# A layer-0 and attention kernel on one core: TensorE's first, middle and last step from searched lists, group two's layer-0 products among the first norms, and one due time for the last chains

## The chip, the cores and the metric

One Trainium2 chip, of which the kernel uses one core. The metric is the device time of one execution in microseconds (us); less is better. All arithmetic is fp32. A core has TensorE (PE in the profile; PEld is its weight load), VectorE (DVE), ScalarE (ACT), GpSimd (POOL) and SyncE (SP, which issues the DMAs here). TensorE writes into PSUM, which has eight banks of 128 x 512 fp32 numbers; the other engines read and write them too.

## The reference

The input x holds 128 graphs of 128 nodes with 512 features. adj is one 128 x 128 matrix, the same for all graphs, with many zeros.

```python
# layer 0
A = einsum('od,bdn->bon', adj, x);  C = A + b[None, :, None]
x = layernorm(x + max(relu(A[:, :, None, :] + (C - A)[:, :, :, None]), axis=-1))
# layer 1: 8 heads of 64
q, k, v = split(x @ w_qkv)
p = softmax(where(adj == 0, -inf, q @ k.T / 8))
o = (p @ v) @ w_proj + b_proj
x = layernorm(x + o + layernorm(o) * ln_gamma + ln_beta)
```

In layer 0 the maximum over the last axis comes down to one number for each node: the largest entry of its row of adj @ x, plus its bias, and no less than 0. So layer 0 costs a product, a row maximum and a norm for each graph.

## The kernel before

**Tiling.** The 128 graphs make 32 groups (`NG`) of `G` = 4. A step p of the main loop (L1297) works on four groups at once (p-1 to p+2), in a software pipeline. Its parts, by the letters that the changed program's lists use too:

- A0 to A3 (`attend`, L1156): probabilities times V for the four graphs of group p-1; ScalarE copies each result out of its bank (L1177).
- S0 to S3 (`scores`, L1034, and `softmax`, L1053): scores of the four graphs of group p, two banks for each graph. VectorE adds the mask and takes the maximum, ScalarE makes eight exponentials (L1087, one for each head, with the row sums) and eight scalings by 1/sum (L1116). Where `on_vector` is true, VectorE scales instead. VectorE transposes in 32 x 32 pieces (L1128), and a DMA out to a DRAM tile (`hop`) and one DMA in for each of four quarters finish the transposition.
- V1 to V7 and O1 to O7 (`Unit`, L880): the V projection of group p and the output projection of group p-1, as Strassen-like schemes of seven products of half size. GpSimd makes four sums of the left operand first. Products add up in four banks; between them ScalarE takes snapshots of a bank (`u`, L919), and VectorE combines bank and snapshot into the result. O's banks 0 and 2 start from a copy of the bias by ScalarE (`seed`).
- L0 to L3 (`l0_mm`, L444): layer-0 products adj @ x of group p+2, each with a row maximum on VectorE; after them come the group's statistics (`bn`, L464), roots and shifts (`finish`, L469, GpSimd), the norm on ScalarE (`norm`, L531), the transposition of x through VectorE and DRAM (`xhop`), and the spill of x with beta added.
- Q0 to Q25 (`qk_unit`, L772): q and k of group p+1, by a bilinear scheme of 26 products (`NODES`). GpSimd makes sums of x (`token_sums`) for it. Between products ScalarE copies a bank into another that goes on from there (a seed, L806) or into a snapshot (L810), and VectorE and GpSimd combine at the end.
- `tails` (L1200): for group p-1, both layer norms, the residual and the store, with x reloaded from the spill.

**The first step** (L1248 to L1295) is written out: layer 0 of group 0, here called I0 to I3, with a norm for each graph; TensorE transposes of its x (X0 to X3, `l0_transpose_pe`, L603), each copied out by ScalarE or VectorE; its q and k by plain products (D0 to D7, `qk_plain`, L719, 16 matmuls each); the layer-0 products of group 1, here J0 to J3; and fillers (`keep_warm`, L365: matmuls on zeros whose result nobody reads). **The last step** (L1351 to L1461) is written out as well: there is no next group, so the attentions of the last group (here B0 to B3), the plain output projection of its graphs (`project`, L1419, here R0 to R3, four 128 x 512 matmuls each on a bank that `seed_last` has filled with the bias) and the chains behind (`tail_before`, L1392, for graphs of the group before, here T0 to T3; `tail`, L1429; both end in `outer`, L1408: statistics, roots on GpSimd, norm on ScalarE, store) close the program.

**TensorE's order** is that of the calls. Before the change it is:

```
first:  K3 T K1 I0 K1 I1 K1 I2 K1 I3 K2 X0 X1 D0 D1 D2 D3 X2 X3 J0 J1 D4 D5 J2 J3 D6 D7 S0 S1 S2 S3
        V1 V2 L0 L1 V6 V5 V4 V7 L2 L3 V3 Q0 ... Q25
middle: A0-A3 S0-S3 V1 V2 L0 L1 V6 L2 L3 V5 V4 V7 O1 O2 V3 O6 O5 O7 O4 Q0 Q1 O3 Q2 ... Q25
last:   A0-A3 S0-S3 V1 V2 V6 V5 V4 V7 O1 O2 V3 O6 O5 O4 O7 B0 O3 B1 T0 R0 B2 T1 R1 B3 T2 R2 T3 R3
```

(K with a number: that many fillers; the first K3 and T, the transpose of adj, are the same in both programs. The Ts in the last row put no work on TensorE; they stand where their chains are added to the plan.)

**The other engines' order** comes from `Plan` (L160). Every operation is recorded with its engine, a cost and what it reads and writes. `schedule` (L221) goes backwards from TensorE and gives each operation a due time: the latest end that leaves its successors in time. An operation without a successor (a store, mostly) is due 9.0 (`BEHIND`) after the planned start of the TensorE operation that was added last before it. Then each engine takes, of what is ready, what is due first. SP's queue, the DMA issues, is ordered in the same way. The program is emitted in that order, and each engine runs its own instructions in it.

**Banks** are assigned by hand: lists X and Y of four banks change places through `FREED` (L131), `Unit` has a table `BANK`, and each row of `NODES` names its bank. A product into a bank waits until whoever reads the old content is done. Snapshots of the q/k scheme go to the buffers u0 to u5 by a table (`SNAP`, L133).

Of the kernel before, what the change touches and what calls it, by code (L numbers as in the profile page):

```python
# [2 lines left out]

# [78 lines left out]
    (((8, 0),), 0, 3, (2,), (), None),  # L82
    (((12, 1),), 2, 6, (), (19,), None),
    (((14, 2),), 1, 4, (8,), (), None),
    (((1, 3), (10, 4)), 0, 5, (), (7,), None),
    (((5, 5), (15, 6)), 1, 9, (7,), (), None),
    (((9, 7),), 0, 25, (10,), (), None),
    (((11, 8),), 2, 14, (12,), (), None),
    (((17, 9),), 4, 11, (20,), (), None),
    (((13, 10),), 3, 13, (), (16,), None),  # L90
    (((16, 11),), 1, 17, (), (12,), None),
    (((18, 12),), 5, 19, (), (11,), None),
    (((19, 13),), 4, 16, (), (15,), None),
    (((5, 14),), 6, None, (), (), 6),
    (((20, 15),), 3, 23, (18,), (), None),
    (((7, 16),), 2, 15, (), (19,), None),
    ((), 2, None, (), (), 7),
    (((6, 17),), 4, None, (), (), 4),
    (((21, 18),), 1, 21, (), (24,), None),
    (((22, 19),), 6, 22, (), (25,), None),  # L100
    (((23, 20),), 5, None, (), (), 3),
    (((24, 21),), 7, 24, (), (22,), None),
    (((0, 22),), 1, None, (), (23, 22), None),
    ((), 6, None, (), (), 1),
    (((25, 23),), 3, None, (), (), 5),
    (((1, 24),), 7, None, (), (), 2),
    (((2, 25),), 0, None, (), (), 0),
# [23 lines left out]
FREED = [2, 4, 5, 6, 1, 3, 7, 0]  # L131

SNAP = {1: 0, 3: 1, 8: 2, 9: 3, 10: 4, 11: 5, 14: 1, 17: 4, 18: 3, 20: 5, 21: 2}  # L133
# [26 lines left out]
class Plan:  # L160
# [32 lines left out]
    ROUNDS, KEPT, BEHIND = 6, 0.5, 9.0  # L193
# [27 lines left out]
    def schedule(self, ideal):  # L221
        ops = self.ops
        for op in reversed(ops):
            ahead = op.lag + (self.AHEAD_DMA + 1.5 * op.kb / self.KB_PER_US if op.kb else self.AHEAD)
            if op.succs:
                due = min(s.due - (0.0 if s.eng == op.eng == "PE" else ahead) for s in op.succs)
            else:
                due = ideal.get(op.after, 0.0) + self.BEHIND
            if op in ideal:
                due = min(due, ideal[op] + op.cost)  # L230
# [61 lines left out]
def kernel(  # L292
# [43 lines left out]

    def halves(b):
        return b.t.rearrange("p (k n) -> p k n", k=2)
# [24 lines left out]
    idle = bank(7)  # L363

    def keep_warm(n):  # L365
        def emit():
# [3 lines left out]
        plan.add("PE", 0.43 * n, emit, [zeros], [idle])  # L370

# [39 lines left out]
    load(2)  # L411
    load(3)
# [15 lines left out]
    pt0 = bank(6)  # L428
    plan.add("PE", 0.4, lambda: pin(PE.transpose(pt0.t[:, :P], adj_sb.t, ident.t)), [adj_sb, ident], [pt0])
    adj_done = plan.add("DVE", 0.25, lambda: pin(V.tensor_copy(adjT.t, pt0.t[:, :P])), [pt0], [adjT])  # L430
    mask = buf("mask", [P, P])
# [12 lines left out]
    def l0_mm(f, k):  # L444
        b = bank(k)
# [16 lines left out]
        )  # L462

# [139 lines left out]
    def l0_transpose_pe(f, k):  # L603
        g, c4 = divmod(f, G)
        h, j = divmod(c4, 2)
        b = bank(k)
# [8 lines left out]
        for half in range(2):  # L615
# [10 lines left out]
            else:  # L626
                plan.add("DVE", 0.4, lambda ops=operands: pin(V.tensor_copy(*ops())), [b], at)

# [18 lines left out]
    def block(i):  # L647
        k, n = divmod(i, 4)
        return raw[n], lambda: raw[n].t[:, k]

    def weight_forms():
        made = {}
        room = ("z", "xr0", "xr1")
        temp_bufs = [buf(s, [P, 4, HE]) for s in room]

        def operand(i):
            if i < 16:
                b, ap = block(i)
                return b, None, ap
# [33 lines left out]
        for w, terms in enumerate(FORMS):  # L693
# [3 lines left out]
            dst, at = (lambda w=w: wqk.t[:, w]), (wqk, w)  # L697
            if len(terms) == 1:
                (i, s), = terms
# [4 lines left out]
                    lambda ap=ap, dst=dst, s=s: pin(A.mul(dst(), ap(), float(s))),  # L704
# [6 lines left out]
            add(dst, at, operand(i), operand(j), si, sj)  # L711
            for i, s in terms[2:]:
                add(dst, at, (wqk, w, dst), operand(i), 1, s)

    def qk_bufs(g):
        for h in range(2):
            qk[g, h] = buf(f"qk{h}", [P, 4, 2, HT])

    def qk_plain(h, banks, eng, ns):  # L719
# [787 lines left out]
```

## Time and profile before

| | |
|---|---|
| device time, median of 3 runs | 1888.86 us (1888.54 to 1889.1) |
| profiled execution, device time | 1889.46 us |
| its span, first to last instruction | 1887.7 us |
| granted TensorE clock, mean | 0.997 |
| TensorE busy | 1865.2 us (99%), 11299 instructions |
| VectorE, ScalarE, GpSimd busy | 1328.0, 1484.1, 1543.4 us (70, 79, 82%) |
| moved by DMA | 341.89 MB, 181 GB/s |
| TensorE busy in 0 to 20 us | 17.52 of 20 (DMA share 0.95) |
| TensorE busy in 60 to 100 us | 36.82 of 40 |
| TensorE busy in 1700 to 1800 us | 100.00 of 100 |
| TensorE busy in 1860 to 1888 us | 12.99 of 28 (granted clock 0.82) |

Rows of the profile read like this. A group's row has the line of the code, the engine, the operation, `out<-in` by tile names (k is a bank, u a snapshot, hl and x1T operands of the projections, s probabilities), the shapes, and how many. In a timeline a row begins with its start and its length in us and gathers neighbours of one form (`x32`); brackets at its end hold the idle time before it and what ended that, as in `[1.39 <-ACT k L806]`: 1.39 us idle until ScalarE's copy of line 806 into k was there. The chain of waits is followed back from the last instruction, at each step to what released it. A table of windows has one row for each stretch: its length, then the busy time (and instructions) of PE, PEld, DVE, ACT and POOL, the granted clock, the DMA share and GB/s. L353 stands for every matmul, L347 and L350 for GpSimd's and VectorE's additions. A 128 x 256 fp32 matmul leaves two records on TensorE, 0.2155 us apart.

### The profile page before, as it was taken

To read this page: it belongs to the slowest core of one execution; us is meant where nothing else is said; L and a number is where in the kernel's file an instruction comes from. 1 tells how busy PE (TensorE), PEld (TensorE's weight loads), DVE (VectorE), ACT (ScalarE), POOL (GpSimd) and SP (SyncE) were. 2 spreads that over 40 slices of the span, in tenths; PEclk is the share of its full clock that TensorE was granted. 3 is DMA by queue.
4 is the path that set the end of the run, shared out by engine and by line. 5 is a ranking of instruction groups with operands and counts; after the bars stand their busy time and mean duration, and the time that the engine had idled before them with its cause. 6 is when DMAs were issued, how large, how long until landed. Compare 5 with 4: busy or idle time off the path is not lost.

```text
span 1887.7 us, 35406 instructions
## 1 busy us (share of the span) xinstructions
PE 1865.2 (99%) x11299; PEld 1592.8 (84%) x11299; DVE 1328.0 (70%) x2432; ACT 1484.1 (79%) x4377; POOL 1543.4 (82%) x1600
## 2 busy tenths in 40 slices
PE   9999999999999999999999999999999999999996
PEld 7788888888888888888888888888888888888884
DVE  6967766776766777667767667676676776776667
ACT  2677778987778877788878798787887878888875
POOL 5668988889888888888797888878888888888884
PEclk9999999999999999999999999999999999999998
DMA  6765677557675666766576756668575766757554
GB/s 210 181 179 130 180 212 201 153 166 192 183 219 165 171 172 180 211 191 155 172 184 192 208 146 190 172 190 213 159 184 160 201 190 190 174 155 198 173 185 156
DMA packets 444857, 341.89 MB, mean 181 GB/s; under 512 B 276736, under 2 KB 378240, under 8 KB 444672
## 3 DMA queue, kind: packets, MB, share of 16 engines
q1 hardware_dynamic: 444384, 339.11, 64.9%
q8 instruction: 91, 1.49, 0.3%
q14 instruction: 94, 0.77, 0.1%
q10 hardware_dynamic: 288, 0.52, 0.1%
HBM read 172.82 MB, written 166.72 MB: 180 GB/s over the span
## 4 chain that ended last, share of the span: by engine, by line
PE 96%; ACT 1%; POOL 1%; DVE 1%; issue 0%; DMA 0%; SPq 0%; POOLq 0%; ACTq 0%
PE k L353 96%; ACT s L1116 0%; ACT s L1087 0%; POOL rs L347 0%; DVE st L466 0%; ACT k L806 0%; DMA s<-hop 0%; SPq L357 0%; POOL x L347 0%; POOL hl L347 0%; ACT z L537 0%; POOL rs L478 0%; ACT u L810 0%; POOL sh L486 0%; DVE pu L1128 0%
## 5 line engine op out<-in xcount | busy, mean ns | idle before, releaser
L353 PE MATMUL k<-hl,wqk 128*128 128x256 f32 x2232 | 517.7, 379 | 1.4 <-ACT k L806 1.4
L353 PEld LDWEIGHTS k<-hl,wqk 128*128 128x128 f32 x2232 | 423.6, 190 | 60.4 <-issue 2.5
L1087 ACT ACTIVATE s<-s,nm 128x128 f32<-128x128 f32 x1024 | 397.1, 391 | 76.4 <-DVE nm L1078 72.9
L1116 ACT ACTIVATE s<-s,rec 128x128 f32<-128x128 f32 x992 | 312.5, 392 | 0.0
L347 POOL TENSOR_TENSOR hl<-x1T 128x512 f32<-128x512 f32 (+1 forms) x250 | 216.6, 874 | 81.4 <-PE k L353 73.1
L353 PE MATMUL k<-x1T,wqk 128*128 128x256 f32 x992 | 244.8, 379 | 3.0 <-ACT u L810 1.6
L350 DVE SCALAR_TENSOR_TENSOR qk<-k,u 128x512 f32<-128x512 f32 x248 | 169.9, 688 | 109.5 <-PE k L353 73.4
L810 ACT COPY u<-k 128x512 f32<-128x512 f32 x341 | 195.6, 584 | 58.9 <-PE k L353 33.9
L353 PE MATMUL k<-wv,hl 128*128 128x256 f32 x1024 | 241.4, 379 | 0.0
L353 PEld LDWEIGHTS k<-wv,hl 128*128 128x128 f32 x1024 | 194.5, 190 | 52.2 <-issue 16.7
L353 PE MATMUL k<-wp,so 128*128 128x256 f32 x992 | 224.5, 379 | 0.0
L353 PEld LDWEIGHTS k<-x1T,wqk 128*128 128x128 f32 x992 | 188.3, 190 | 29.3 <-ACT u L810 2.0
L350 DVE SCALAR_TENSOR_TENSOR s<-k,mask 128x512 f32<-128x512 f32 x256 | 158.3, 683 | 77.8 <-PE k L353 75.1
L353 PEld LDWEIGHTS k<-wp,so 128*128 128x128 f32 x992 | 188.4, 190 | 25.7 <-issue 0.2
L347 POOL TENSOR_TENSOR hl<-x1T,hl 128x512 f32<-128x512 f32 (+1 forms) x249 | 197.5, 807 | 0.2 <-DMA x1T<-xhop 0.2
L1087 ACT ACTIVATION_READ_ACCUMULATOR s<-s,nm 128x1 f32 x1024 | 194.3, 190 | 0.0
L919 ACT COPY u<-k 128x512 f32<-128x512 f32 x189 | 110.6, 586 | 101.7 <-PE k L353 96.1
L347 POOL TENSOR_TENSOR x<-x,be_bc 128x1024 f32<-128x1024 f32 x62 | 146.4, 2361 | 46.4 <-DVE xt L572 27.2
L353 PE MATMUL k<-wv,x1T 128*128 128x256 f32 x768 | 179.5, 383 | 0.0
L1128 DVE STREAM_TRANSPOSE pu<-s 128x1024 f32<-128x1024 f32 x128 | 158.2, 1236 | 27.1 <-ACT s L1116 27.0
L353 PE MATMUL k<-wp,oT 128*128 128x256 f32 x744 | 170.7, 379 | 0.0
L347 POOL TENSOR_TENSOR z<-z,ga_bc 128x1024 f32<-128x1024 f32 x60 | 142.0, 2366 | 29.1 <-ACT z L537 29.1
(138 smaller groups left out, 3366.6 us busy)
## 6 DMA issues: line engine op xcount, KB each, us to landing
hop<-pu SPq DMA_DIRECT2D x128, 512.0 KB, 2.7
s<-hop SPq DMA_DIRECT2D x512, 128.0 KB, 3.7
spill<-x SPq DMA_DIRECT2D x62, 512.0 KB, 4.8
xhop<-xt SPq DMA_DIRECT2D x248, 128.0 KB, 2.8
x1T<-xhop SPq DMA_DIRECT2D x248, 128.0 KB, 4.9
x<-in_x_dram SPq DMA_DIRECT2D x60, 512.0 KB, 5.1
xr<-spill SPq DMA_DIRECT2D x60, 512.0 KB, 5.3
out_dram<-xr SPq DMA_DIRECT2D x60, 512.0 KB, 5.1
```

Source lines behind the costliest of these rows:

```text
L347: pin(eng.tensor_tensor(dst, a, b, op))
L350: pin(V.scalar_tensor_tensor(dst, a, s, b, op0, op1))
L353: pin(PE.matmul(dst, lhsT=lhsT, rhs=rhs, start=start, stop=True, skip_group_check=True))
L810: plan.add("ACT", 0.5, lambda b=b, u=u: pin(A.copy(u.t, b.t)), [b], [u])
L919: plan.add("ACT", 0.5, lambda: pin(A.copy(u.t, b.t)), [b], [u])
L1087: A.activation(flat()[:, i], flat()[:, i], AF.Exp, bias=nm.t[:, i : i + 1], accum_out=sm.t[:, i : i + 1],)
L1116: A.activation(flat()[:, i], flat()[:, i], AF.Identity, scale=rec.t[:, i : i + 1])
L1128: V.transpose(u.t.rearrange("p q h b -> p h q b"), flat().rearrange("p h (q a) -> p h q a", q=Q),)
```

## The change

The three orders become lists that a search produced; one loop over all 32 steps reads them token by token. `FIRST` is step 0 (K, I, J, X, D, S, V, L, Q), `STEP` the middle steps (steps whose group p+2 doesn't exist drop their L), `LAST` step 31 (A, S, V, O, B, T, R). Each token is added to the plan where it stands, with all that hangs on it: S with its softmax, T and R with their chains, and `tails(p - 1)` right after O3. J0 to J3, layer 0 of the second group, now stand between the products, norms and transposes of the first (I, X, D0, D1). There are 6 fillers in place of 9, the three ahead of T included.

Banks are no longer named: `take` hands out the one that has been free longest, and `give` returns a bank as soon as the last reader is recorded. `NODES` loses its bank column, `SNAP` becomes a queue of the six buffers, `Unit` becomes `Strassen` (each product brings its snapshot and results, in any order), `qk_unit` becomes `Bilinear`. In the last step the bias copy into R's bank is added with each R, where before all four stood ahead of B0.

In `schedule` an operation without a successor that would be due within `EQUAL` = 12.0 of the end is due at the end (TensorE's planned end + 9.0), the same for all of these. The outer norm of the last graph goes to VectorE (`on_vector`: GpSimd makes only the root; one VectorE instruction subtracts the mean and multiplies), where the others have a shift on GpSimd and a norm on ScalarE. The loads of x for pairs 2 and 3 are split in two DMAs each.

Instructions as recorded in the plan, before and after: TensorE 1662 and 1660 operations, VectorE 2432 and 2433, ScalarE 3354 and 3353, GpSimd 1451 and 1449, SP 1414 and 1416.

```diff
-    (((8, 0),), 0, 3, (2,), (), None),
-    (((12, 1),), 2, 6, (), (19,), None),
...
+    (((8, 0),), 3, (2,), (), None),
+    (((12, 1),), 6, (), (19,), None),
...
-FREED = [2, 4, 5, 6, 1, 3, 7, 0]
-
-SNAP = {1: 0, 3: 1, 8: 2, 9: 3, 10: 4, 11: 5, 14: 1, 17: 4, 18: 3, 20: 5, 21: 2}
...
+STEP = """
+A0 A1 A2 A3 S0 S1 S2 S3 V1 V2 L0 L1 V6 V5 O1 O2 V7 L3 L2 V4 O6 V3 O5 O7 O4 Q0 O3 Q2 Q3 Q1 Q4 Q5 Q6
+Q7 Q8 Q9 Q10 Q11 Q12 Q13 Q14 Q15 Q17 Q16 Q19 Q20 Q18 Q21 Q22 Q24 Q25 Q23
+""".split()
+
+FIRST = """
+K1 I0 K1 I1 I2 J0 K1 J1 I3 X0 X1 J2 D0 X2 D1 J3 X3 D3 D2 D6 D4 S1 S0 D5 D7 V1 V4 L0 L1 S3 V6 V5 L2
+V7 V2 V3 Q0 Q1 S2 L3 Q2 Q3 Q4 Q5 Q8 Q9 Q6 Q17 Q10 Q7 Q12 Q14 Q21 Q13 Q11 Q19 Q20 Q23 Q18 Q15 Q24 Q25
+Q16 Q22
+""".split()
+
+LAST = """
+A0 A1 S0 A2 S1 A3 V1 S2 S3 O1 V5 V6 V4 O5 O2 V7 O6 O7 O4 T3 V3 V2 B0 B1 O3 T2 T1 T0 R0 R1 B2 B3 R3
+R2
+""".split()
...
-    ROUNDS, KEPT, BEHIND = 6, 0.5, 9.0
+    ROUNDS, KEPT, BEHIND, EQUAL = 6, 0.5, 9.0, 12.0
...
+        end = max(op.cost + t for op, t in ideal.items()) + self.BEHIND
...
             else:
                 due = ideal.get(op.after, 0.0) + self.BEHIND
+                if due > end - self.EQUAL:
+                    due = end
...
+    free = deque(range(8))
+
+    def take():
+        return bank(free.popleft())
+
+    def give(b):
+        free.append(int(b.slot[1:]))
...
-    load(2)
-    load(3)
+    load(2, None, True)
+    load(3, None, True)
...
+            banks = self.banks
+            self.add(i, (None, 0, 1, 2, 3, 2, 0, 0)[i])
+            if i in (1, 6, 7):
+                self.snap((1, 6, 7).index(i) + 1)
+            if i == 2:
+                self.result(0, 0, 1, 1)
+                give(banks[1])
+            elif i == 7:
+                give(banks[0])
+                self.result(1, 1, 2, 3)
+            elif i == 3:
+                self.result(0, 1, 2, 2)
+                give(banks[2])
+            if i in (4, 7) and 3 in banks and 3 in self.snaps:
+                self.result(1, 0, 3, 3)
+                give(banks[3])
...
+    def outer(b, zk, z, mz, on_vector=False):
         bn(z, [zk], mz, 0)
-        (st,) = finish(mz, range(1))
-        norm(z, z, st, [zk], [zk])
+        if on_vector:
+            rs = root_only(mz, range(1))
+            plan.add(
+                "DVE",
+                0.65,
+                lambda: pin(
+                    V.tensor_scalar(
+                        z(), z(), mz.t[:, 0, 0:1], rs.t[:, :1], ALU.subtract, ALU.mult
+                    )
+                ),
+                [zk, mz, rs],
+                [zk],
+            )
+        else:
...
+    for p in range(NG):
+        a, f = G * p, G * (p + 2)
+        step = FIRST if p == 0 else STEP if p < NG - 1 else LAST
+        if f >= B:
+            step = [t for t in step if t[0] != "L"]
+        last = {t[0]: i for i, t in enumerate(step)}
+        v = o = q = None
+        if p == NG - 1:
+            again = reload_last(p)
+        for i, t in enumerate(step):
+            kind, n = t[0], int(t[1:])
+            if kind == "K":
+                keep_warm(n)
+            elif kind == "I":
+                l0_mm(n)
+                xb, j = xs[n // 2], n % 2
+                bn(lambda xb=xb, j=j: xb.t[:, j], [(xb, j)], mv0, n, [adj_done])
+                l0_norm_one(0, n, finish_first(mv0, n, rcol[0]))
+            elif kind == "J":
+                l0_mm(G + n)
+            elif kind == "X":
+                l0_transpose_pe(n)
+            elif kind == "D":
+                h, n = divmod(n, 4)
+                if (0, h) not in qk:
+                    qk[0, h] = buf(f"qk{h}", [P, 4, 2, HT])
+                qk_plain(h, copies, [n])
+            elif kind == "A":
+                attend(a - G + n)
+            elif kind == "S":
+                softmax(a + n, scores(a + n), p == 0 and n >= 2 or p == NG - 1 and n < 2)
+            elif kind == "L":
+                l0_mm(f + n)
+            elif kind == "B":
+                attend(a + n)
+            elif kind == "T":
+                tail_before(a - G + n)
+            elif kind == "R":
+                project(a + n, i == len(step) - 1, *again)
+            elif kind == "V":
+                v = v or v_unit(p)
+                v.product(n)
+            elif kind == "O":
+                o = o or o_unit(p - 1)
+                o.product(n)
+                if n == 3 and p < NG - 1:
+                    tails(p - 1)
+            else:
+                if q is None:
+                    token_sums(p + 1)
+                    q = Bilinear(p + 1)
+                q.node(n)
+            if p == 0 and i == max(last["I"], last["X"]):
+                for q0 in range(2):
+                    l0_beta_spill(q0)
+                load(4)
+                load(5)
+            if p == 0 and i == max(last[k] for k in "IJXD"):
+                xT0 = x1T[0]
+                xT0.log = [(o, k[0] if type(k) is tuple else k, w) for o, k, w in xT0.log]
+                group_l0(1, [[0, 1], [2, 3]])
+                weight_forms()
+                weight_load(wp, w_proj, 0)
+                ga_bc = broadcast("ga_bc", ln_gamma)
+                bp_bc = broadcast("bp_bc", b_proj)
+                weight_sums(wv)
+                weight_sums(wp)
+                bd = buf("bd", [P, HE])
+                plan.add("POOL", 0.8, bias_gap, [bp_bc], [bd])
+            if f < B and i == max(last["L"], last["V"]):
+                group_l0(p + 2, [[0, 1, 2, 3]])
+                for qn in (2 * (p + 3), 2 * (p + 3) + 1):
+                    if qn < NQ:
+                        load(qn)
 
     for op in plan.run(3.0):
         op.emit()
```

## The prediction, made before the changed kernel ran

> **What bounds the kernel now.** I read the page's chain of work first, then the same chain in order of time, then TensorE's timeline at both ends. The page's chain:
>
> ```profile
> PE 96%; ACT 1%; POOL 1%; DVE 1%; issue 0%; DMA 0%; SPq 0%; POOLq 0%; ACTq 0%
> ```
>
> In order of time, its long pieces (start, length, what):
>
> ```profile
> 14.28 14.08 PE k L353 x64
> ...
> 95.17 11.96 PE k L353 x108
> 107.22 1696.07 PE k L353 x10320
> 1803.31 0.57 ACT k L806
> ```
>
> From 107.2 to 1803.3 us the chain never leaves TensorE. A busy share does not say whether matmuls run back to back, so I took starts from the timeline: a record of a 128x256 fp32 matmul (each matmul has two) starts 0.2155 us after the one before, and in the 29 middle steps (p = 1 to 29) no record starts over 0.15 us late. A middle step is 56.5 us of matmul. The change moves matmuls there and removes none: **the middle can only lose**. What can be won lies before 107 and after 1803. TensorE's timeline there:
>
> ```profile
> 12.63 0.66 PE L611 MATMUL k<-ident,x 128*128 128x128 f32 x4 [0.31 <-ACT x L537]
> 14.28 7.17 PE L353 MATMUL k<-x1T,oT 128*128 128x256 f32 x32 [0.99 <-DVE x1T L627]
> ...
> 71.29 6.21 PE L353 MATMUL k<-hl,wqk 128*128 128x256 f32 x28
> 78.89 1.10 PE L353 MATMUL k<-hl,wqk 128*128 128x256 f32 x4 [1.39 <-ACT k L806]
> ...
> 81.55 1.03 PE L353 MATMUL k<-x1T,wqk 128*128 128x256 f32 x4
> 84.19 1.13 PE L353 MATMUL k<-x1T,wqk 128*128 128x256 f32 x4 [1.61 <-ACT u L810]
> ```
>
> From start to start these waits cost 28 x 0.2155 = 6.03, so 78.89 - 71.29 - 6.03 = 1.57, and likewise 1.78; the released copies are ScalarE's, which the windows (length, then each engine's busy time) show idle, then full:
>
> ```profile
> 20.00:36.00 16.00, 16.00 (x76) 13.39 (x75) 11.47 (x20) 1.92 (x4) 10.49 (x9) 1.00 0.51 166
> 36.00:60.00 24.00, 24.00 (x151) 19.70 (x150) 19.82 (x36) 8.04 (x24) 17.70 (x19) 1.00 0.57 138
> 60.00:84.00 24.00, 21.18 (x92) 16.76 (x90) 22.54 (x41) 23.62 (x82) 15.67 (x22) 1.00 0.55 158
> ```
>
> ScalarE (third from last of the busy times) has 1.92 of 16, then 8.04 of 24, then 23.62 of 24 us.
>
> **Start, up to the first query/key projection D0 (14.28 us now).** Units, start to start: a filler 0.43, a layer-0 product 0.86 (four records took 1.72 at 29.07), a transpose X 0.43, D 3.45, V and O 1.73, Q 0.862, scores S 0.94, attention A 0.91. Fillers fall from 9 to 6. Up to the second layer-0 product I1 at 7.41 both programs are equal. Then the changed list has I1, I2, J0, K, J1, I3, X0, X1, J2: 6 x 0.86 + 3 x 0.43 = 6.45, to 13.86. D0 also needs VectorE's two copies of X0 and X1. VectorE's queue there: maxima of I1 and I2 from 8.47 (0.69 each, 0.60 apart), the small steps of both norms to 10.9, one maximum (J0), one statistics row (0.68), then I3's maximum, which waits for I3 (12.14) and ends about 13.0, then two copies (0.42) to 13.85. ScalarE's norms (0.81) end at 12.3, before X1 is due at 12.57. So **D0 at 13.9**, with three J products (2.58) already done that now stand at 29.07 and 37.69: 0.38 + 2.58 = **2.96 won**. Bounds: 1.7 (two more VectorE rows slip ahead of the copies) to 3.0 (TensorE's own list). x is loaded before the weights; 2.1 MB must land before D0, and the DMA records have 2.2 MB landed by 9.0 us, so the loads hide; the two more SP issues (0.43 each) stand in a queue that is ahead there.
>
> A rule speaks against fewer fillers. The row first: fillers start 0.43 us per record apart up to 6.87 us and 0.2155 after, though the granted clock reads 1.00 throughout. The Trainium skill, "TensorE: Matmul & The Clock Gate", Part 1, says that the array is gated to half rate until about 3.4 us of activity and again after an idle window as long. By it a filler too few could cost half a window, an estimate of 1.7 us. The trace has 1.3 us of waits around 12.6 to 14.3 and full pitch after; the changed list has no longer gap.
>
> **First step, up to A0 (92.15 us now).** From 14.28 the list (8 D, X2, X3, 4 J, 4 S, 7 V, 4 L, 26 Q) is 73.6 us; with the two waits that makes 91.2, so 0.9 are small gaps, 0.18 of it one wait at 66.5. From 13.9 without three J: 71.0, and 0.75 of gaps: A0 at 85.65. The two waits go if ScalarE can be earlier, and this is what the list does: S1 and S0 start after six D, two X and J3, 13.9 + 22.4 = 36.3, where all four S now start at 46.41; S3 at 50.3; S2 only at 62.4. A graph's softmax costs ScalarE 8 exponentials (0.385 apart) and, for two graphs, 8 scalings (0.305): 11 of the 16 us fall into time that is idle now. Adding up ScalarE's queue in its new order, the tightest copies for the Q products end 0.0, 0.4 and 0.8 us before they are needed: I take 0.2 of waits. Next in line is the third attention (87.5): S2's softmax ends on ScalarE about 71.7, then VectorE 0.20 + 1.37 + 1.24, the hop out (0.34 + 2.7) and in (four issues, 3.7): 84 to 85, hidden with 2.5 us to spare; so the 0.3 that A3 waits at 95.17 goes too. Sum: 3.35 + 0.18 + 0.3 - 0.2 = **3.6 won**. Bounds 0 (the queue only shifts) to 4.
>
> **The middle: 0.** Banks now go round in the order in which they are freed. I counted places in one step where a product follows within about 2 us of the ScalarE or VectorE work that it waits for (under 1.3 us spare): 7 now, 5 after. Adding up ScalarE's queue with its rows (0.50 a copy, 0.385, 0.305, 0.72 a norm), the latest copy has 0.37 us left in both orders; VectorE 1.6 now, 1.1 after; GpSimd over 4 in both. Layer-0 maxima, sums, hops and loads keep counts and lengths; their covers are tens of us. Price if the 0.37 goes: 29 times what is missing. Below zero is excluded, since matmuls are back to back.
>
> **Step 30, last step.** Waits now, start to start (1.53, 0.84, 0.89, 0.41: 3.67):
>
> ```profile
> 1802.25 7.07 PE L353 MATMUL k<-hl,wqk 128*128 128x256 f32 x32
> 1810.69 1.13 PE L353 MATMUL k<-x1T,wqk 128*128 128x256 f32 x4 [1.37 <-ACT k L806]
> ...
> 1852.24 1.09 PE L353 MATMUL k<-s,v 128*64 128x128 f32 x16 [0.68 <-ACT u L919]
> ...
> 1865.30 1.09 PE L353 MATMUL k<-s,v 128*64 128x128 f32 x16 [0.73 <-DMA s<-hop]
> ...
> 1870.27 3.70 PE L353 MATMUL k<-wqk,oT 128*128 128x512 f32 x8 [0.25 <-ACT oT L1177]
> ```
>
> The second is the price of a bank copied and reused at once: 0.84 for a 0.59 copy. LAST has that three times: O7 straight after O6 in one bank (0.84), R3 straight after B3, whose copy it reads (0.84), and B0 straight after V2, whose 0.69 VectorE result it reads (0.95): 2.6. The hop's wait goes (S3 is some 31 us ahead of B3). Step 30 keeps its full ScalarE (9.6 to 9.7 us in each 10 from 1782); its queue puts two norms and eight scalings ahead of copies, about 0.9 late. 3.5 against 3.67: **0.1 won** (-2 to +1.5).
>
> **Tail.** TensorE ends at 1873.97, the span at 1887.7: 13.7 us. The rows that decide:
>
> ```profile
> 1876.48 0.69 DVE L466 BATCH_NORM_STATS2 st<-k 128x6 f32<-128x512 f32 x1
> 1880.80 0.69 DVE L466 BATCH_NORM_STATS2 st<-z 128x6 f32<-128x512 f32 x1
> 1883.99 0.81 ACT L537 ACTIVATE z<-z,sh,rs 128x512 f32<-128x512 f32 x1
> ```
>
> The last product's statistics wait 2.5 us behind other graphs' rows; its second statistics end at 1881.49, 7.5 after TensorE; then 3.3 through GpSimd (two other roots first) and ScalarE, then 2.9 for the store. In the change T3 and part of T2 come before the last products, and the common deadline lets the last graph's rows stand earlier: after TensorE's end VectorE has about ten rows (0.60 to 0.72), 6.6; then 0.2 + 0.25 + 0.57 + gaps = 1.2, and the new VectorE normalisation, not in the trace: between a copy (0.68) and the two-operation row (0.75), I take 0.75, nearest in work; store 2.9. 11.5: **2.2 won** (0 if roots or rows queue as now, to 4).
>
> **Sum:** 2.96 + 3.6 + 0 + 0.1 + 2.2 = 8.9. The profiled execution took 1889.46, 0.60 over the median 1888.86: 1880.6 for a profile, **1880.0** for the median.
>
> **Rivals.** (1) The first step's waits stay: S2 is late, ScalarE is full to 78 us either way, and the 3.4 come back as other waits: 1883.4. For it: a slack of 0.0 in my sum; against: 11 us of work moved into idle time. (2) The ends give nothing: the three tight pairs cost more where ScalarE is late (each delayed copy adds itself), and VectorE, full from O3 on, keeps the tail at 13.7, so that the deadline does not do what it says: 1882.3 to 1885. (3) Slower: in the middle the seeded copy with 0.37 us left falls behind one norm (0.72) and one exponential (0.385): 0.73 a step, 29 times, 21: 1901. It decides from 0.31 a step (no gain left) and 0.44 (slower). Against it: the same 0.37 costs nothing now, and there are fewer tight places.
>
> **Chances.** What a measurement of this kernel can tell from no change is about 0.2%, 3.8 us: 1885.1 to 1892.6. Forecast (1876 to 1882.3) 0.60; rival 1 0.12; rival 2 0.13; rival 3 0.15, of which 0.07 stays inside 0.2% and 0.08 is slower. Faster 0.85, same 0.07, slower 0.08. The low end takes all upper bounds (3.0 + 4 + 1.5 + 4 = 12.5); the high end takes in rivals 1 and 2: 1876 to 1885.5.
>
> **What would show it.** D0 at 13.9 (+-0.4) and J products before it; no ScalarE-released wait over 0.5 us between 60 and 85; A0 near 85.7; one unbroken TensorE piece from about 90 to about 1795; waits of 0.8 to 1.0 before O7, B0 and R3; TensorE's end near 1867.3 and 11 to 12 us after it. I am wrong if waits recur with a period near 56 us, if D0 comes after 15, or if the tail is still over 13.

## The result, and the profile after

| | before | changed |
|---|---|---|
| device time, median of 5 runs | 1888.86 us (1888.37 to 1889.76) | 1881.57 us (1880.88 to 1882.49) |
| ratio | | 0.9961, 95% interval 0.9947 to 0.9976 |
| profiled execution, and its span | 1889.46, 1887.7 | 1882.49, 1879.6 |
| D0 starts | 14.28 | 13.29 |
| A0 starts (first step's end) | 92.15 | 88.40 |
| A0 of the last step | 1821.43 | 1816.00 |
| TensorE's last end | 1873.97 | 1869.47 |
| from there to the span's end | 13.71 | 10.13 |

The kernel became 7.3 us faster; the forecast was 8.9. The single terms differ from their forecasts by more than the sum does. Counted between these marks, start to start, in the two profiles:

| term | forecast | measured | how |
|---|---|---|---|
| start: D0, and three J products done before it | 2.96 | 3.57 | 14.28 - 13.29, and 3 x 0.86 |
| first step, from D0 to A0, and the waits up to the next A0 | 3.6 | 0.90 | 77.88 - 2.58 - 75.12 = 0.18; first period 58.39 to 57.67 = 0.72 |
| middle | 0 | 0.17 | one period of 57.84 became 57.67 like all others |
| step 30 and last step | 0.1 | -0.16 | period of step 30 56.06 to 55.27; A0 to TensorE's end 52.53 to 53.48 |
| tail | 2.2 | 3.58 | 13.71 - 10.13 |

Together they make 8.06, the difference of the spans. The time around the span was 1.1 us longer in this profile than in that of before, so its whole time differs by 6.97 only. Lines of kernel.py have moved: L380 stands for every matmul here, L374 and L377 for GpSimd's and VectorE's additions, and in the runs below they shift by a few lines.

The chain of waits of the changed kernel, in order of time (start, length, what), is again one piece of TensorE through the whole middle. What stands ahead of it is new:

```profile
31.44 4.23 DVE wqk L374 x3
35.67 4.23 DVE xr L374 x3
...
42.24 2.39 DVE s L377 x4
...
61.56 1737.95 PE k L380 x10610
```

In the first step the chain lies on VectorE's weight forms (`z`, `xr` and `wqk` at L374), 128x256 additions of which three took 4.23 us. TensorE's timeline shows what this does. The waits of 1.6 and 1.8 us among the Q products are gone; three others stand among the V products:

```profile
51.78 3.69 PE L380 MATMUL k<-wv,hl 128*128 128x256 f32 x16 [0.42 <-ACT u L936]
...
56.81 1.99 PE L380 MATMUL k<-wv,hl 128*128 128x256 f32 x8 [0.48 <-ACT u L936]
...
61.56 1.97 PE L380 MATMUL k<-wv,hl 128*128 128x256 f32 x8 [1.03 <-POOL hl L374]
```

Start to start they are 0.63, 0.65 and 1.19 us, 2.47 in all. The first two wait for ScalarE's snapshots. The third is put down to GpSimd's `hl`, but that sum was done at 39.3; what came last is VectorE's combination of the bank that V3 goes on in with a third snapshot, V7's, of 60.16: the first of the three in this row (60.77 to 61.46):

```profile
60.77 1.88 DVE L374 TENSOR_TENSOR v<-k,u 128x512 f32<-128x512 f32 x3
```

ScalarE's rows say why the snapshots are late:

```profile
40.26 0.57 ACT L767 COPY qk<-k 128x512 f32<-128x512 f32 x1
45.80 0.40 ACT L1084 ACTIVATE s<-s,nm 128x128 f32<-128x128 f32 x1 [4.98 <-DVE nm L1075]
...
51.07 0.56 ACT L936 COPY u<-k 128x512 f32<-128x512 f32 x1
```

S1's scores end at 36.9, but its maxima (`nm`) come at 45.7: ScalarE stands idle for 4.98 us, and then the exponentials lie in front of the snapshot that V6 needs. VectorE's masks for S1 and S0 came at 42.17 to 44.6, behind the forms.

In the last step the three tight pairs cost somewhat more than they were expected to (0.84, 1.20, 0.90 start to start, forecast 0.84, 0.95, 0.84):

```profile
1840.79 2.00 PE L380 MATMUL k<-wp,so 128*128 128x256 f32 x8 [0.67 <-ACT u L936]
...
1849.00 1.97 PE L380 MATMUL k<-s,v 128*64 128x128 f32 x32 [1.03 <-DVE v L374]
...
1862.34 7.13 PE L380 MATMUL k<-wqk,oT 128*128 128x512 f32 x16 [0.68 <-ACT oT L1174]
```

And the end of VectorE's timeline answers to the tail of before. The last product's statistics (1869.90) wait 0.4 us after TensorE's end, not 2.5, and the last row is the new normalisation:

```profile
1869.90 0.66 DVE L497 BATCH_NORM_STATS2 st<-k 128x6 f32<-128x512 f32 x1
...
1876.00 0.55 DVE L1301 TENSOR_SCALAR z<-z,mvm,rs 128x512 f32<-128x512 f32 x1 [1.06 <-POOL rs L374]
```

### The profile page after: what moved, and what is told of

It reads as the page before. It is cut to its first block, busy times and chain, and to the rows that moved or that the text cites. A ratio compares the mean times of both kernels' runs of the same rounds, so it can differ in the third digit from the quotient of the medians.

```text
span 1879.6 us, 35324 instructions
## 1 busy us (share of the span) xinstructions
PE 1863.4 (99%) x11293; PEld 1594.2 (85%) x11293; DVE 1323.9 (70%) x2433; ACT 1475.6 (79%) x4376; POOL 1542.1 (82%) x1598
## 4 chain that ended last, share of the span: by engine, by line
PE 96%; DVE 2%; POOL 1%; issue 0%; ACT 0%; POOLq 0%; DVEq 0%; ACTq 0%
PE k L380 96%; DVE wqk L374 1%; DVE st L497 0%; POOL hl L374 0%; POOL z L374 0%; DVE xr L374 0%; POOL rs L374 0%; DVE z L374 0%; DVE s L377 0%; POOL o L374 0%; DVE qk L771 0%; PE k L642 0%; DVE z L377 0%; DVE nm L1075 0%; POOL wp L374 0%
## 5 line engine op out<-in xcount | busy, mean ns | idle before, releaser
L380 PE MATMUL k<-hl,wqk 128*128 128x256 f32 x2232 | 522.4, 380 | 0.6 <-ACT k L844 0.4
L380 PEld LDWEIGHTS k<-hl,wqk 128*128 128x128 f32 x2232 | 424.6, 190 | 58.7 <-issue 1.2
L1113 ACT ACTIVATE s<-s,rec 128x128 f32<-128x128 f32 x992 | 306.3, 391 | 0.0
L377 DVE SCALAR_TENSOR_TENSOR qk<-k,u 128x512 f32<-128x512 f32 x248 | 169.7, 686 | 109.3 <-PE k L380 55.9
L380 PE MATMUL k<-x1T,wqk 128*128 128x256 f32 x992 | 244.5, 380 | 0.0
L374 POOL TENSOR_TENSOR hl<-x1T 128x512 f32<-128x512 f32 (+1 forms) x250 | 216.4, 871 | 33.3 <-PE k L380 33.3
L847 ACT COPY u<-k 128x512 f32<-128x512 f32 x341 | 192.2, 581 | 60.6 <-PE k L380 33.3
L380 PE MATMUL k<-wv,hl 128*128 128x256 f32 x1024 | 237.0, 380 | 1.9 <-POOL hl L374 1.0
L380 PE MATMUL k<-wp,so 128*128 128x256 f32 x992 | 229.7, 380 | 0.7 <-ACT u L936 0.7
L380 PEld LDWEIGHTS k<-wv,hl 128*128 128x128 f32 x1024 | 194.7, 190 | 41.6 <-issue 8.7
L380 PEld LDWEIGHTS k<-wp,so 128*128 128x128 f32 x992 | 188.6, 190 | 26.5 <-ACT u L936 1.1
L380 PEld LDWEIGHTS k<-x1T,wqk 128*128 128x128 f32 x992 | 188.7, 190 | 25.6 <-DVE wqk L374 0.3
L377 DVE SCALAR_TENSOR_TENSOR s<-k,mask 128x512 f32<-128x512 f32 x256 | 156.5, 681 | 72.8 <-PE k L380 72.8
L374 POOL TENSOR_TENSOR hl<-x1T,hl 128x512 f32<-128x512 f32 (+1 forms) x249 | 196.0, 803 | 0.1
L380 PE MATMUL k<-wv,x1T 128*128 128x256 f32 x768 | 179.6, 384 | 0.0
L380 PEld LDWEIGHTS k<-wv,x1T 128*128 128x128 f32 x768 | 143.6, 190 | 34.1 <-issue 14.0
L380 PE MATMUL k<-wp,oT 128*128 128x256 f32 x744 | 171.0, 380 | 0.0
L1174 ACT COPY oT<-k 128x512 f32<-128x512 f32 x128 | 75.0, 586 | 118.8 <-PE k L380 118.6
L374 POOL TENSOR_TENSOR x<-x,be_bc 128x1024 f32<-128x1024 f32 x62 | 146.3, 2360 | 19.0 <-ACT xr L568 13.1
```

Of the source, the lines that this page charges most:

```text
L374: pin(eng.tensor_tensor(dst, a, b, op))
L377: pin(V.scalar_tensor_tensor(dst, a, s, b, op0, op1))
L380: pin(PE.matmul(dst, lhsT=lhsT, rhs=rhs, start=start, stop=True, skip_group_check=True))
L847: plan.add("ACT", 0.5, lambda: pin(A.copy(u.t, b.t)), [b], [u])
L1113: A.activation(flat()[:, i], flat()[:, i], AF.Identity, scale=rec.t[:, i : i + 1])
L1174: lambda: pin(A.copy(dst.t[:, :, ts(jj, P)], bk.t.rearrange("p (c n) -> p c n", c=KC))),
```

## The experiments

All start from the changed kernel. Marks are taken from each run's profile. Where no range is given, the time is that of one execution; the kernel before took 1889.0 to 1890.3 us beside these.

**What is the first step bound by?** Two kernels. The first takes the early scores back and keeps the new start:

```diff
 FIRST: "K1 I0 K1 I1 I2 J0 K1 J1 I3 X0 X1 J2
-        D0 X2 D1 J3 X3 D3 D2 D6 D4 S1 S0 D5 D7 V1 V4 L0 L1 S3 V6 V5 L2 V7 V2 V3 Q0 Q1 S2 L3 Q2 ...
+        D0 D1 D2 D3 X2 X3 J3 D4 D5 D6 D7 S0 S1 S2 S3 V1 V2 L0 L1 V6 V5 V4 V7 L2 L3 V3 Q0 ... Q25
```

> The changed kernel with FIRST cut down to its start: I, J, K, X as in the changed list up to D0 (J3 after X3), and from there the order of before (D0 to D3, X2, X3, D4 to D7, all four S, then V, L, Q in order). Theory 'VectorE' (the early scores bring nothing, since their maxima wait behind weight forms on VectorE and their exponentials then stand in the way of V's snapshots; the whole gain of the first step is the start): D0 at 13.3 to 13.9, the two waits of 1.6 and 1.8 us of before at Q products are back, A0 at 88.4 +- 0.7, time 1881 to 1883. Rival 'as predicted' (the early scores do free ScalarE and are worth 3 us, and some other new wait ate that): A0 at 89.5 to 92, time 1883 to 1886.

Measured: 1886.34 us, D0 at 14.38, A0 at 92.37, both marks and the time a little past what either theory said. 'VectorE' was the theory I held after reading the result, and it fell: without the early scores the first step is 2.9 us longer from D0 to A0 (77.99 for 75.12). But the waits of before do not come back either; one other does, and it is not ScalarE's:

```profile
79.80 1.03 PE L378 MATMUL k<-hl,wqk 128*128 128x256 f32 x4
83.99 1.10 PE L378 MATMUL k<-hl,wqk 128*128 128x256 f32 x4 [3.17 <-DVE wqk L372]
85.31 3.56 PE L378 MATMUL k<-hl,wqk 128*128 128x256 f32 x8 [0.21 <-DVE wqk L372]
```

Here the weight forms themselves are late on VectorE. And the eight records from 85.31 take 3.56 us, where four of the same form took 1.03 just before the wait. The window (length, busy time of PE, PEld, DVE, ACT, POOL, granted clock, DMA share, GB/s) shows the clock:

```profile
80.00:84.00 4.00, 0.83 (x5) 0.42 (x3) 4.00 (x4) 1.62 (x3) 4.00 (x3) 1.00 0.96 254
84.00:89.00 5.00, 4.79 (x13) 3.64 (x14) 5.00 (x12) 0.68 (x2) 0.97 (x1) 0.66 0.71 222
```

After 3.3 us without work TensorE ran at half pitch (the next record starts twice as late as usual) for some 3.7 us, which cost about 1.8 more. So much of the 2.9 us is this one wait and what follows it, and the run does not price the early scores by themselves.

The second kernel leaves all lists alone. In the changed kernel's trace, GpSimd adds two SBUF operands from 24.65 to 39.3 (mostly sums of `wv` for V, then `hl`), and beside it most of VectorE's forms take 1.4 us each:

```profile
31.11 2.86 POOL L374 TENSOR_TENSOR hl<-x1T 128x512 f32<-128x512 f32 x2
```

```profile
31.03 0.41 DVE L374 TENSOR_TENSOR z<-oT,so 128x256 f32<-128x256 f32 x1
31.36 1.48 DVE L374 TENSOR_TENSOR wqk<-wqk,z 128x256 f32<-128x256 f32 x1
32.77 1.49 DVE L374 TENSOR_TENSOR wqk<-z 128x256 f32<-128x256 f32 x1
...
39.49 0.41 DVE L374 TENSOR_TENSOR xr<-oT,oT 128x256 f32<-128x256 f32 x1
```

The plan's code has GpSimd's sums after the forms, but nothing on the chip makes GpSimd wait for that. One column copied from the last early form, ahead of GpSimd's second sum, does:

```diff
     for op in plan.run(3.0):
+        if op is held:
+            pin(GP.tensor_copy(gate.t, wqk.t[:, 14, :1]))
         op.emit()
```

> The changed kernel with one tiny GpSimd copy (one column of the last early weight form) ahead of GpSimd's second sum for V, so that GpSimd's sums start after VectorE's weight forms as the plan has it, and no longer beside them. Theory 'shared' (a 128x256 VectorE addition takes 0.34 us alone and 1.4 beside GpSimd's additions, and these 5 to 7 us are what makes the early maxima late): forms done by about 33 instead of 42, masks of S1 at 37 to 38 instead of 42.2, the three waits in V (0.63, 0.65 and 1.19 us, 2.5 in all) fall under 0.8 in all, A0 at 86.0 to 87. Rival 'list' (the V waits come from the order of V products and ScalarE's queue, whenever the softmax starts): forms faster, but waits of 2 us or more in V stay, A0 at 88 to 89. A third outcome: GpSimd's sums become late and V6 waits for them, A0 over 89.

Measured: 1879.11 us. D0 to A0 fell from 75.12 to 72.63, and all three waits in V are gone. VectorE's rows in this run: the forms 0.34 apart, the last at 32.71, and VectorE idle until the scores are there.

```profile
32.37 0.41 DVE L374 TENSOR_TENSOR wqk<-oT,xr 128x256 f32<-128x256 f32 x1
32.71 0.42 DVE L374 TENSOR_TENSOR wqk<-wqk,xr 128x256 f32<-128x256 f32 x1
37.39 2.48 DVE L377 SCALAR_TENSOR_TENSOR s<-k,mask 128x512 f32<-128x512 f32 x4 [4.27 <-PE k L380]
```

The exponentials start at 41.03 instead of 45.80, and the V1 snapshot at 47.12, as soon as its product ends. No list and no engine's order was changed, so this is shown: the V waits come from the two engines' additions slowing each other. The Trainium skill, "SBUF — State Buffer", section "Who interferes with whom", says that a VectorE instruction with two SBUF inputs contends with a GpSimd instruction that reads SBUF, and that the loser waits for the whole instruction. These rows agree: 1.4 us is the length of one GpSimd addition beside VectorE's (2.86 for two), and 0.34 is the distance of VectorE's rows without.

Timed in five rounds:

> The kernel sums_after_forms again, timed: the changed kernel with the tiny GpSimd copy that holds back GpSimd's sums. Theory 'shared': 1879.1 +- 0.6 us median, 2.3 to 2.9 under the changed kernel's 1881.57, A0 at 72.6 after D0. Rival 'chance' (the single run was low because TensorE reached its full pitch early): D0 to A0 is 74 or more and the median within 1 us of 1881.57.

Measured: median 1878.92 us (1878.66 to 1879.54), ratio to before 0.9947 (0.9934 to 0.9961); D0 to A0 72.64. All its runs lie under all five of the changed kernel. With one added instruction the program is faster than both kernels. What was not run is the order of before with GpSimd held back, so how much of this needs the early scores is open.

**Do the tight pairs of the last step cost their waits and nothing else?**

```diff
 LAST: "A0 A1 S0 A2 S1 A3 V1 S2 S3 O1 V5 V6 V4 O5 O2 V7
-       O6 O7 O4 T3 V3 V2 B0 B1 O3 T2 T1 T0 R0 R1 B2 B3 R3 R2"
+       O6 V3 O7 V2 O4 T3 O3 B0 B1 T2 T1 T0 R0 R1 B2 B3 R2 R3"
```

> The changed kernel with another LAST: V3 between O6 and O7, O4 and O3 between V2 and B0, R2 between B3 and R3; all else as in the changed list. Theory 'pairs' (the waits of 0.84, 1.20 and 0.90 us at O7, B0 and R3 are the price of three tight pairs alone): they go, nothing comes in their place, A0 of the last step to TensorE's end falls from 53.5 to 50.5 to 51.2 us, time about 1879. Rival 'queues' (the last step is bound by ScalarE's and VectorE's queues; a wait that is taken away at one product comes back at the next): 52.5 to 55 us, with new waits at S0, at an R or at B3, and the time within 1.5 us of the changed kernel's 1881.6 or above it.

Measured: 1883.94 us; A0 to TensorE's end 55.50. My theory was wrong, and the rival right in kind, with half a us more than its 55. The three waits are gone, but S0 waits 0.8 us for GpSimd's `qk`, R1 waits 2.3 us (start to start) for its bias copy, and the clock falls again, for 1.7 us more:

```profile
1857.13 5.40 PE L379 MATMUL k<-wqk,oT 128*128 128x512 f32 x8 [2.09 <-ACT k L1316]
```

```profile
1857.00:1861.00 4.00, 3.87 (x5) 1.65 (x6) 4.00 (x10) 1.56 (x3) 3.77 (x8) 0.57 0.22 65
```

The bias copy waited for VectorE (2.3 us, the trace names `x` at L373), which still read the bank: with eight banks in a queue, a bank comes free only when the chain that used it is through. (Beside TensorE, only VectorE and ScalarE touch banks in the traces of both kernels; GpSimd has no row with one.)

A search for a better LAST, by trial in the plan's own model, gave two lists, both tried with the held-back sums:

> sums_after_forms with a LAST that a small search in the plan's own model found (A2 A0 S0 A1 S2 S1 A3 V1 O1 V6 O5 O7 V5 S3 V4 O6 O4 V2 V7 O2 V3 B0 B1 O3 T1 T2 T3 T0 R1 R0 B2 R2 B3 R3): the plan sees TensorE's end 2.0 us and the last store 2.8 us earlier than with the changed list. Theory 'queues' (the model sees the queues that loose_last ran into): A0 of the last step to TensorE's end 51 to 52.5 us for 53.5, tail 9 to 10.5, median 1876.5 to 1878.5. Rival 'model' (the plan's waits are not the chip's): 53.5 or more, median 1879 or above.

Measured: 1876.52 us (1876.29 to 1877.58), tail 9.10, as theory 'queues' had it; A0 to TensorE's end 52.95, between the two. This list has O7 ahead of O6, so snapshots of O hold other sums and the output of group 30 is another one; the work is the same, but it is no kernel to use. With the order of snapshots kept:

> sums_after_forms with a LAST from a search in the plan's model that keeps the order in which snapshots and results must come (A2 A0 S0 A1 S1 A3 V1 S3 O1 S2 V6 V4 O6 O5 V5 O7 V7 O4 T3 V3 O2 V2 B0 B1 T2 O3 T1 T0 R0 R1 B2 R2 B3 R3); the plan sees TensorE's end 1.8 us and the last store 2.5 us earlier. Theory 'queues': as searched_last, 1 to 2.5 us under sums_after_forms' 1878.92, from waits of under 2.3 us in the last step (2.9 now) and a tail of 9 to 10. Rival 'model': the waits stay at 2.9 us or more, 1878.5 or above.

Measured: 1878.56 us (1877.93 to 1878.95), A0 to TensorE's end 53.83, tail 9.11. The plan had seen 1.8 us less on TensorE, and there was 0.4 more, with waits of 0.99, 0.90 and 0.90 in the last step, 2.8 in all, and one of 1.0 in step 30. That is rival 'model', but for 0.1 us of waits: the model's waits are not the chip's to within a microsecond. The gain in the tail (1.0) is lost on TensorE in part, and its five runs overlap those of sums_after_forms (1878.66 to 1879.54): no difference that can be told.

**What shortened the tail?** Four kernels. Without the common due time:

```diff
-    ROUNDS, KEPT, BEHIND, EQUAL = 6, 0.5, 9.0, 12.0
+    ROUNDS, KEPT, BEHIND, EQUAL = 6, 0.5, 9.0, -99.0
```

> The changed kernel without the common due time (EQUAL out of reach), all lists as they are. Theory 'deadline' (of the 3.6 us that the tail lost, the common due time gives most, since it lets the last graph's rows stand ahead of other chains): the tail after TensorE's end grows from 10.1 to 12 us or more. Rival 'list' (T3 and T2 ahead of the last products, and the norm on VectorE, give it): 10.1 to 10.9 us.

Measured: 1882.44 us, tail 10.23. The due time gives 0.1 us at most: the tail was 9.86 in front_only, where nothing of the last step was changed, so 0.1 cannot be told from nothing. The norm on ScalarE again:

```diff
-                project(a + n, i == len(step) - 1, *again)
+                project(a + n, False, *again)
```

> The changed kernel with the last graph's outer norm on ScalarE again (root, shift and product on GpSimd, norm on ScalarE), lists and due time as changed. Theory 'order': tail 10.6 to 10.9 us (two GpSimd steps of 0.24 and 0.19 with their gaps, and 0.81 for 0.55). Rival 'norm': 12 us or more.

Measured: 1881.88 us, tail 10.95: the norm on VectorE gives 0.8. LAST in the order of before, with the due time and without:

```diff
 LAST: "
-       A0 A1 S0 A2 S1 A3 V1 S2 S3 O1 V5 V6 V4 O5 O2 V7 O6 O7 O4 T3 V3 V2 B0 B1 O3 T2 T1 T0 R0 R1 B2 B3 R3 R2"
+       A0 A1 A2 A3 S0 S1 S2 S3 V1 V2 V6 V5 V4 V7 O1 O2 V3 O6 O5 O4 O7 B0 O3 B1 T0 R0 B2 T1 R1 B3 T2 R2 T3 R3"
```

> The changed kernel with LAST in the order of before (all A, all S, V1 V2 V6 V5 V4 V7 O1 O2 V3 O6 O5 O4 O7 B0 O3 B1 T0 R0 B2 T1 R1 B3 T2 R2 T3 R3); due time and norm on VectorE as in the changed kernel. Theory 'order' (of the 3.6 us that the tail lost, the place of T3 to T0 ahead of the last products gives most): the tail goes back to 12.5 to 14 us; A0 of the last step to TensorE's end 52.5 to 54. Rival 'norm' (VectorE's norm of the last graph, with one GpSimd step less, gives most): tail 10.3 to 11.3 us.

> old_last without the common due time (EQUAL out of reach): the order of before in the last step, the norm of the last graph on VectorE. Theory 'deadline needs the order' (the common due time puts the rows of all late chains on a par, and with T2 and T3 after the last products this sends the last graph behind the others): the tail falls from old_last's 16.8 to 12.4 to 13.2 us, 0.8 under the 13.7 of the kernel before; the place of T3 to T0 in the new list is then worth 2.2 to 3 us of tail by itself. Rival 'order alone' (the long tail comes from the old order in the new queue of banks): 15.5 us or more.

Measured: 1891.27 us with a tail of 16.82, and 1889.26 with 15.12. The first is past the 12.5 to 14 of theory 'order', the second lies between its theory and its rival. So the order of the last step is what the tail lives on: 6.7 us of tail with the due time, 4.9 without. The whole list was put back; the place of T and R was not tried by itself. With the old order the due time makes it 1.7 worse; VectorE then waits 4.05 us for a root that stands behind three other graphs' roots on GpSimd:

```profile
1879.07 0.37 DVE L497 BATCH_NORM_AGGREGATE mvm<-st 128x2 f32<-128x6 f32 x4
1883.49 0.55 DVE L1300 TENSOR_SCALAR z<-z,mvm,rs 128x512 f32<-128x512 f32 x1 [4.05 <-POOL rs L373]
```

The same order had a tail of 13.7 in the kernel before. Why it has 1.4 us more in the new program (2.2 with the norm's 0.8) is not settled; the queue of banks, in which each R's bias is copied only when its bank comes free, was not tried by itself. One thing more: in both runs TensorE waits 1.83 us at the same product of step 30. In old_last half pitch follows and costs 1.7 us; in the other none follows.

**Is the middle touched by the order?**

```diff
 STEP: "
-       A0 ... S3 V1 V2 L0 L1 V6 V5 O1 O2 V7 L3 L2 V4 O6 V3 O5 O7 O4 Q0 O3 Q2 Q3 Q1 ... Q24 Q25 Q23"
+       A0 ... S3 V1 V2 L0 L1 V6 L2 L3 V5 V4 V7 O1 O2 V3 O6 O5 O7 O4 Q0 Q1 O3 Q2 ... Q25"
```

> The changed kernel with STEP in the order of before; FIRST, LAST and the plan as changed. Theory 'middle costs nothing' (TensorE is back to back in both orders): the steps from the third on take 57.67 us each as now, the waits after the first A0 (0.39 and 0.25 in the kernel before) come back in part, and A0 to the last step's A0 is 1727.6 to 1729.3. Rival 'banks' (the new order is what makes the queue of banks work): waits that recur in each step, 0.1 us or more a step, 1730.5 or above.

Measured: A0 to the last A0 is 1729.06, all periods from the second to the step before the last 57.67: the middle costs nothing, as predicted. The whole, though, took 1890.25 us, and not because of the middle. The first step, whose list is the same, grew from 75.12 to 80.64 us, with waits of 1.67 and 3.22 us among the Q products, both for weight forms on VectorE, and half pitch after the second; the last step grew by 1.5 us. The plan places the other engines' work anew whenever any list changes.

**Is half pitch a matter of the wait before it?** It had shown up three times unasked. A forced wait at the start of 14 middle steps:

```diff
+    def stall(k):
+        b, c = take(), take()
+        for last_one in (False, True):
+            plan.add("PE", 0.862, lambda: mm(b.t, adjT.t, bp_bc.t, True), [adjT, bp_bc], [b])
+            if not last_one:
+                for _ in range(k):
+                    plan.add("DVE", 0.61, lambda: pin(V.tensor_copy(c.t, b.t)), [b], [c])
+        give(b)
+        give(c)
```

> The changed kernel with a forced wait of TensorE at the start of 14 middle steps: a product into a bank, then 1, 2, 3, 4, 5, 1, 2, 3, 4, 5, 2, 3, 2, 3 VectorE copies of that bank (0.6 us each), then a second product into it. It computes the same; it is slower by the waits and the 28 products. Theory 'pitch' (an idle time over about 1.7 us puts TensorE at half pitch for 2 to 4 us after it, as behind the waits of 3.2, 2.1 and 1.7 us in front_only, loose_last and old_last): after 1 copy full pitch, after 3 and more half pitch behind each, after 2 (about 1.7 idle) some. Rival 'coincidence' (the half pitch came from what ran beside, or from the place in the program): full pitch after most of the waits, whatever their length.

Measured (1987.27 us): one copy gave waits of 0.96 us and full pitch behind both. With more copies the waits came out longer than meant, since the copies stand in VectorE's queue. All seven waits over 4 us were followed by half pitch, which cost 1.6 to 3.1 us. Of the forced waits between 2 and 4 us, those of 3.14, 3.19 and 3.73 us were followed by it, those of 2.42 and 3.68 were not. The first step had changed too: a wait of 2.65 us there was followed by full pitch, but two of 1.67 and 0.74 us with 0.9 us of work between them by half pitch (at 91.5 us, 1.7 us lost). Here one with, one without (start, length, what; a product is two records):

```profile
941.79 1.02 PE L382 MATMUL k<-bp_bc,adjT 128*128 128x512 f32 x2
947.23 2.07 PE L382 MATMUL k<-bp_bc,adjT 128*128 128x512 f32 x2 [4.41 <-DMA x1T<-xhop]
949.23 4.92 PE L382 MATMUL k<-s,v 128*64 128x128 f32 x64
...
1687.24 1.12 PE L382 MATMUL k<-bp_bc,adjT 128*128 128x512 f32 x2 [3.52 <-DMA spill<-x]
1688.30 3.71 PE L382 MATMUL k<-s,v 128*64 128x128 f32 x64
```

Rival 'coincidence' falls, since ten of the fourteen forced waits were followed by half pitch and no short one was. Theory 'pitch' does not hold as a threshold at 1.7 us; what these few waits show is a chance that is greater after longer waits.

## Why the prediction was right, and where not

The forecast was 1880.0 us, and 1881.57 was measured, inside the range and on the right side. It holds as a sum of terms that erred both ways: the first step gave 2.7 us less than forecast, the start and the tail 2.0 more. That these nearly cancel is luck. Of the signs named, the unbroken middle and the waits before O7, B0 and R3 came; A0 (88.40 for 85.7) and TensorE's end (1869.47 for 1867.3) were late, and the tail (10.1 for 11 to 12) was shorter.

- **Start: right.** Forecast D0 at 13.9 and 2.96 won. In no_deadline, which has the same lists and reached full pitch at the same point as the profile of before (last record at half pitch at 6.66 us in both), D0 is at 13.98: 0.30 and 2.58 make 2.88. The profile of the changed kernel has 0.7 more because full pitch came earlier in it: the last record at half pitch starts at 4.96. That part is chance, not the change. The prediction's 6.87 for the end of half pitch is not the start of any record. The fillers were not missed: by the rule of the Trainium skill ("TensorE: Matmul & The Clock Gate", Part 1), which I weighed against fewer fillers, half pitch could have lasted longer, but in none of the twelve profiles that start with the changed list and six fillers did it last longer than in the one profile of before with nine.
- **First step: wrong.** The step that failed is "11 of the 16 us fall into time that is idle now". (The 16 is 17.2 by the prediction's own figures, and ScalarE's is the second from last of the busy times in its windows, not the third; neither carries the error.) The prediction added up ScalarE's queue and took the maxima for ready when the scores are; VectorE's queue was summed up to D0 only. The maxima came nearly 5 us later than VectorE can give them (exponentials at 45.8, and at 41.0 with GpSimd held back), behind forms of 1.4 us. Of 3.6 us 0.9 came, and 0.7 of that lies in the waits of the next step: from D0 to A0 it was 0.18 of 3.55 (77.88 - 2.58 - 71.75). The trace of before had it. Its forms at 30.6 and 34.7 us took 1.40 and 1.36 beside GpSimd's sums, and those at 23.3 to 24.3 were 0.34 apart without:

```profile
23.64 0.41 DVE L347 TENSOR_TENSOR z<-oT,so 128x256 f32<-128x256 f32 x1
23.97 0.41 DVE L347 TENSOR_TENSOR xr<-so,z 128x256 f32<-128x256 f32 x1
...
30.61 1.40 DVE L347 TENSOR_TENSOR wqk<-so 128x256 f32<-128x256 f32 x1
...
34.69 1.36 DVE L347 TENSOR_TENSOR xr<-so,so 128x256 f32<-128x256 f32 x1
```

With GpSimd held back, D0 to A0 is 72.6; the forecast was 71.75 (85.65 - 13.9). So the forecast of this part holds to 0.9 us once VectorE can follow. Of the 0.9, 0.4 is a price that it left out: in sums_after_forms the scores of two graphs in a row take 1.98 us of TensorE and those of the two single ones 1.10 and 1.09, together 4.17, where the four in a row of before take 3.77.

- **Rival 1 came true in its result** (new waits in the first step for the old ones), not in its mechanism: it had ScalarE full to 78 us, but ScalarE was busy 15.1 of 24 us from 36 to 60 and 17.0 of 24 from there to 84. The time came out under its 1883.4 because the start and the tail gave more.
- **Rival 2** came true in half: the last step lost 0.95 us, but the tail did not stay at 13.7.
- **Middle: right**, 57.67 in every period. Two readings of the prediction are off without harm: a middle step is 57.67 us, not 56.5, and step 1 of the kernel before has records that start 0.44 us (95.17) and 0.25 us (107.22) late, of which it priced one at 0.3.
- **Step 30 and last step: right in the sum** (-0.16 for 0.1). The three pairs were named and priced at 2.6; they took 2.94. That loosening them brings nothing was not foreseen.
- **Tail: right in kind, too small.** 11.5 forecast, 10.1 measured: VectorE's rows after TensorE's end 5.5 us for 6.6, the new normalisation 0.55 for 0.75. Its reason was half wrong: the due time was to let the last graph's rows stand earlier, and it is worth 0.1 at most. The norm is worth 0.8, and the order of the last step more than the rest (4.9 to 6.7 in the new program), against 1.4 to 2.2 us that the old order costs more there than in the kernel before, for a reason that stays open.
- **Rival 3**, the slower middle, did not appear.

## What to carry to other kernels

Before pricing a row, look at what ran beside it: the same 128x256 additions on VectorE stood 0.34 us apart alone and took 1.4 beside additions on GpSimd. When work is moved earlier onto an idle engine, follow the operand back through the engine that feeds it; idle time of ScalarE was no gift while VectorE was late. An order that a plan computes is kept on the chip only within each engine; where one engine's timing depends on another staying off, make it wait, for one small copy here was worth 2.6 us.

## What the runs showed of the hardware

- **A long wait of TensorE costs more than itself.** Waits are counted from start to start. Waits of up to 1.77 us that stood alone were followed by full pitch in every run; two of 1.67 and 0.74 us close together, in stalls, were not. Of two waits of 1.83 us at the same product (old_last and old_last_no_deadline), one was followed by half pitch, the other not. After 2.26, 3.14 to 3.33 and 3.73 us, and after all seven over 4, matmuls ran at half pitch for 3.3 to 6.2 us, 1.6 to 3.1 us were lost, and the granted clock was 0.50 to 0.83 in windows of 4 to 6 us around them; after 2.01, 2.42, 2.65 and 3.68 us there was nothing of it. The Trainium skill ("TensorE: Matmul & The Clock Gate", Part 1) has the clock fall after an idle window of about 3.4 us, and the window run freely. That some waits of 1.8 to 2.3 us are enough differs from the first part; that equal waits end differently agrees with the second.
- **The same start takes 12.6 to 14.0 us.** In the twelve profiles of programs with the changed list up to D0 (front_only left out) the first matmul starts at 1.17 us, but the last record at half pitch starts between 3.46 and 6.67 us, and D0 goes with it: 12.61 for 3.46 (loose_last), 13.29 for 4.96 (the changed kernel), 13.98 for 6.66 (no_deadline). That is 1.4 us of time that no change to the kernel explains; marks later in the program should be counted from D0.
